# ACT in the order of the program for two of three attention sweeps of a transformer block

## The chip, the cores and the metric

The kernel runs on one core of one Trainium2 chip. The metric is device time in microseconds (us), the median of several executions; the kernel before took 2492.71 us (three runs, 2482.8 to 2496.35). The engines are named as in the profile: PE (TensorE, with PEld for its weight loads), DVE (VectorE), ACT (ScalarE), POOL (GpSimd) and SP (SyncE, which here only issues DMA transfers). Each engine takes its instructions from one queue of its own, in the order in which the built program lists them.

## The reference

All data are float32. The input is x of 2048 rows (tokens) by 1024. With `norm` a layer norm without weights:

```
xn = norm(x)
q, k, v = xn @ wq.T + bq, xn @ wk.T + bk, xn @ wv.T + bv    # each 2048 x 32 heads x 32
scores  = einsum('shd,std->sht', q, k) / sqrt(32)            # 32 x 32 for each token: heads attend to heads
context = einsum('sht,std->shd', softmax(scores), v)
x = x + context
dq = nf4_quant_dequant(w)         # w1, w2: 2752 x 1024, w3: 1024 x 2752
x = x + (silu(norm(x) @ dq1.T) * (norm(x) @ dq2.T)) @ dq3.T
```

`nf4_quant_dequant` works on blocks of 64 weights: it divides by the largest absolute value of the block, replaces each value by the nearest of 16 fixed codes, and multiplies back.

## The kernel before, in words

**The stages.** Three sweeps come first, one for q, one for k and one for v. Each goes over 8 pairs of 128-token tiles, 16 tiles in all. Then a "plain" block of 8 matmul groups (the first weight tile of the feed-forward) is woven with the last context work, and then the feed-forward runs over groups of weight tiles.

**One product.** Every pair of tiles in a sweep is one call of `products` (line 348). It is a Strassen product: seven block products instead of eight. One block product is four matmuls (`mm4`, line 337; the profile shows each fp32 matmul as two records, so eight of them under L339). The sums that Strassen needs are made by letting PE go on accumulating in one PSUM bank `z` and copying it at intermediate points: ACT copies `g0` after the first block product into z, `u2` after the second, `u4` after the third (`copied`, L358); `s7` is a copy of the other bank, `q`. The order on PE is z, q, z, r, z, z (or y), q. PE may not accumulate further into z until the copy of the value before is done. In the first sweep the sixth block product goes to a bank of its own, y, so nothing waits for u4 there; in the other two it goes to z, and ACT copies the end result (`ce`, L383). DVE adds the parts to the two outputs ce and co (L375, L379, L387, L390).

**What else a product carries.** Between block products `fill(n)` puts other work into the program:

- First sweep: PE transposes the normalised x of the next pair (16 transposes `pt`, L471) after the fifth block product, in four groups of four with three PSUM banks. ACT copies each bank twice: to `A` (L474) and, with other strides, to `AV` (L475), which the v sweep will use. DVE forms the Strassen differences of both (L396 to L399), and SP stores them to DRAM (opD, L482; opV, L486). There is one AV buffer: its next copy must wait for the store. DVE also transposes q and adds the bias (L403, L404), and forms Strassen differences of the k and v weights (L516 to L519).
- Second sweep: the scores of the pair before (`sc`, 32 x 32 matmuls in parts of 64, L419), then max, subtraction, exp (ACT, `pr`, L583), sum and scaling.
- Third sweep: the context (`cx`, L433), in parts of 64 matmuls into one PSUM buffer; DVE transposes it back (L652), adds x (L656), SP stores the residual (x1d, L658), and DVE normalises x in the same buffer (L116, L117, L334), which so waits for the store. Two products later PE transposes it (L694), ACT copies that (`xT`, L695), DVE makes differences (`xU`, L710), and SP stores these for the feed-forward.

**The quantiser.** A generator, `background` (line 219), runs through all three stages and the feed-forward. It works on one weight tile of 128 x 1024 after another. A tile has 15 steps. Twelve of them are one ACT activation `sg` (L242) and one DVE operation on `r` (L243); three are DVE alone (L234, L236, L238). There are two sg buffers, so ACT can be at most two steps ahead of DVE. In front of a tile stand an absolute maximum (DVE, L207), a reciprocal (L214, L215) and 16 scalings of 64 columns on ACT (`wn`, L195); at its end 16 more scalings on ACT (`r`, L195). After that the tile is transposed by PE (`ptw`, L161), copied by ACT (`wop`, L162) and stored for the feed-forward (`finish`, line 147). `advance(n)` takes n steps of the generator at that place of the program, `flush` half of a tile's transposes. A product of the first sweep takes 7 steps, one of the third sweep 9. The first feed-forward units need the first tiles; `until` makes sure that they come before.

**What sets the order.** A scheduler orders the instructions of each engine. It takes them from the program, gives each the priority of its place there, and runs a model of the engines: an engine takes whatever instruction is ready, the earliest first. The order that comes out is fixed in the built program. Engines named to `manual_schedule` are excepted: their instructions stay in the order in which the program has them. Before the change that is PE alone, from the beginning to the end. The quantiser's steps depend on little, so where the model sees ACT and DVE idle the scheduler takes them earlier than the program has them.

## Time and profile before

| | us |
|---|---|
| median of three runs | 2492.71 |
| the profiled execution | 2491.25 |
| its span, first to last instruction | 2489.5 |
| PE busy | 2385.8 |
| DVE busy | 1982.1 |
| ACT busy | 1610.2 |
| POOL busy | 279.8 |
| granted clock of PE, mean | 0.987 |

Boundaries in that execution, by PE's first matmul of each stage: first sweep 12.7, second 246.4, third 535.5, plain block 779.5, feed-forward about 832, end 2489.5.

How to read the rows: a timeline row has the start in us from the span's beginning, the duration, the engine, the source line, the operation, the output and input by the program's names (buffer numbers left out), sizes, and how many were merged; in brackets the idle time of the engine before it and what ended it. A row of waits has the engine and what it was to do, whom it waited for, the total in us, how often, and the longest. A waiting engine that isn't PE costs nothing by itself.

### The profile page before, as it was taken

The numbers are of one execution on the slowest core, as the hardware profiler recorded it, in microseconds if no ns is written. First come the engines' busy times: TensorE is split into PE (matmuls) and PEld (weight loads), VectorE is DVE, ScalarE is ACT, GpSimd is POOL, SyncE is SP. The second block draws the span as 40 slices with busy tenths as digits, with TensorE's granted clock in tenths as the row PEclk, the third lists the DMA queues.
The fourth block names the chain that finished last, engine by engine and source line by source line (L and its number), as shares of the span: only waits on it lengthen the run. The fifth ranks groups of instructions, "written<-read, shape, count | busy, mean of one in ns | idle before, by whom it ended". The sixth has DMA issues, their size and how long they took to land.

```text
span 2489.5 us, 36718 instructions
## 1 busy us (share of the span) xinstructions
PE 2385.8 (96%) x14000; PEld 1119.6 (45%) x14000; DVE 1982.1 (80%) x2208; ACT 1610.2 (65%) x3267; POOL 279.8 (11%) x352
## 2 busy tenths in 40 slices
PE   7999999999899999999999999999999999899998
PEld 4444455545455444444444444444444444344433
DVE  7999788878988588989888899898988979871022
ACT  3556544444553378898888988889888888871200
POOL 1010000000000012030120301203012030120300
PEclk8999999999999999999999999999999999999999
DMA  8788643656669587394973939739496394872973
GB/s 309 280 315 327 239 161 116 231 210 218 215 226 324 195 292 166 110 199 148 327 163 119 199 145 323 170 110 207 154 293 174 128 198 157 283 152 72 198 268 138
DMA packets 177297, 513.90 MB, mean 206 GB/s; under 512 B 15904, under 2 KB 70176, under 8 KB 154720
## 3 DMA queue, kind: packets, MB, share of 16 engines
q1 hardware_dynamic: 136224, 438.08, 48.5%
q0 software_dynamic: 40320, 73.42, 18.2%
q8 instruction: 110, 1.80, 0.3%
q14 instruction: 67, 0.55, 0.1%
q10 hardware_dynamic: 576, 0.05, 0.0%
HBM read 283.69 MB, written 227.80 MB: 205 GB/s over the span
## 4 chain that ended last, share of the span: by engine, by line
DVE 18%; issue 17%; ACT 14%; PE 14%; DMA 4%; POOL 1%; DVEq 0%; SPq 0%; POOLq 0%; ACTq 0%
DVE r L243 11%; ACT sg L242 5%; PE z L339 5%; ACT wn L195 4%; PE z L976 4%; DMA x1d<-acc 3%; ACT acc L988 2%; ACT r L195 2%; PE y L976 2%; PE q L339 2%; PE r L976 1%; PE rr L339 1%; POOL x1d L990 1%; DMA out_dram<-acc 1%; ACT wop L162 1%
## 5 line engine op out<-in xcount | busy, mean ns | idle before, releaser
L243 DVE SCALAR_TENSOR_TENSOR r<-sg,r 128x1024 f32<-128x1024 f32 x780 | 945.8, 1214 | 98.1 <-ACT sg L242 66.8
L242 ACT ACTIVATE sg<-wn 128x1024 f32<-128x1024 f32 x780 | 812.4, 1053 | 307.0 <-DVE r L243 286.6
L990 POOL DMA_DIRECT2D x1d<-acc x280 | 244.5, 879 | 1285.7 <-ACT acc L988 1160.8
L339 PE MATMUL z<-xB,w 128*128 128x512 f32 x720 | 324.4, 600 | 5.2 <-ACT u L909 3.7
L339 PE MATMUL z<-xT,w 128*128 128x512 f32 x656 | 296.3, 594 | 5.4 <-ACT u L902 5.4
L339 PE MATMUL q<-xT,w 128*128 128x512 f32 x656 | 291.6, 592 | 0.0
L195 ACT ACTIVATE wn<-wn,rc 128x64 f32<-128x64 f32 x1032 | 267.4, 341 | 22.3 <-DVE rc L215 22.3
L976 PE MATMUL z<-w,h 128*128 128x512 f32 x496 | 236.8, 604 | 2.2 <-DMA w<-wd 1.7
L339 PEld LDWEIGHTS z<-xB,w 128*128 128x128 f32 x720 | 135.4, 192 | 172.4 <-issue 154.7
L339 PEld LDWEIGHTS z<-xT,w 128*128 128x128 f32 x656 | 121.7, 190 | 155.0 <-issue 136.9
L339 PEld LDWEIGHTS q<-xT,w 128*128 128x128 f32 x656 | 123.4, 190 | 149.4 <-issue 146.6
L339 PE MATMUL q<-wT,A 128*128 128x512 f32 x384 | 174.7, 598 | 3.0 <-DVE A L398 3.0
L339 PE MATMUL z<-wT,A 128*128 128x512 f32 x384 | 175.5, 600 | 1.8 <-ACT u L358 1.5
L976 PE MATMUL y<-w,h 128*128 128x512 f32 x320 | 153.9, 599 | 14.7 <-DVE h L963 12.7
L339 PE MATMUL z<-wB,A 128*128 128x512 f32 x320 | 153.0, 623 | 13.4 <-ACT u L358 13.2
L195 ACT ACTIVATE r<-r,am 128x64 f32<-128x64 f32 x608 | 155.1, 341 | 15.6 <-DVE r L243 15.2
L339 PE MATMUL rr<-xB,w 128*128 128x512 f32 x328 | 147.5, 592 | 0.0
L976 PEld LDWEIGHTS z<-w,h 128*128 128x128 f32 x496 | 93.7, 194 | 113.3 <-issue 98.1
L207 DVE TENSOR_REDUCE am<-wn 128x16 f32<-128x1024 f32 (+1 forms) x65 | 78.4, 1206 | 59.0 <-ACT r L195 53.2
L988 ACT COPY acc<-z 128x512 f32<-128x512 f32 x160 | 93.2, 582 | 35.7 <-PE z L976 31.7
L339 PEld LDWEIGHTS q<-wT,A 128*128 128x128 f32 x384 | 72.6, 192 | 91.1 <-issue 84.8
L339 PEld LDWEIGHTS z<-wT,A 128*128 128x128 f32 x384 | 70.4, 190 | 80.7 <-issue 77.1
(132 smaller groups left out, 2591.4 us busy)
## 6 DMA issues: line engine op xcount, KB each, us to landing
x1d<-acc POOLq DMA_DIRECT2D x280, 256.0 KB, 6.1
wd<-wop SPq DMA_DIRECT2D x31, 2048.0 KB, 7.2
w<-wd SPq DMA_DIRECT2D x41, 1280.0 KB, 7.6
wn<-in_w_dram SPq DMA_DIRECT2D x63, 512.0 KB, 4.7
xT<-xdT SPq DMA_DIRECT2D x28, 1024.0 KB, 8.0
xB<-xdB SPq DMA_DIRECT2D x24, 1024.0 KB, 6.1
w<-wd SPq DMA_DIRECT2D x42, 512.0 KB, 5.1
w<-wd SPq DMA_DIRECT2D x10, 1536.0 KB, 7.7
```

What stands on the lines that cost most here:

```text
L162: nc.scalar.copy(o[:q, first + half], pt[:q])
L195: nc.scalar.mul(dst[:, ts(n, BLOCK)], src[:, ts(n, BLOCK)], by[:, n : n + 1])
L207: nc.vector.tensor_reduce(am[:, :nb], v.rearrange("p (b e) -> p b e", e=BLOCK), AX.X, ALU.max, apply_absolute_value=True,)
L242: nc.scalar.activation(t, v, AF.Copy, bias=-edge * by, scale=by)
L243: nc.vector.scalar_tensor_tensor(r, t, code, r, ALU.min, ALU.max)
L339: nc.tensor.matmul(dst, w[:, k, :], xop[:, k, :], start=start and k == 0, stop=stop and k == 3, skip_group_check=True,)
L976: nc.tensor.matmul(dst, side[n][:, ts(q, P)], w3T[g[2 * m]][:, W3[n]], start=start and m == 0, stop=stop and m == 1, skip_group_check=True,)
L988: nc.scalar.copy(t, src)
L990: nc.gpsimd.dma_start(x1d[8 * tbp + 2 * q + j][n], t, accum_op=ALU.add)
```

## The change

A helper `order` is added, which ends the present exception from scheduling and opens a new one for the engines given. It is called four times: PE and ACT before the first sweep, PE alone before the second, PE and ACT before the third, and PE alone before the plain block. So in the first and third sweep ACT executes exactly in the order in which the program is written; in the second sweep, the plain block and the feed-forward the scheduler orders ACT as before. No instruction is added or removed, and no buffer changes. DVE, SP and POOL stay with the scheduler throughout.

```diff
-    ctx.enter_context(tc.manual_schedule(engines={nc.tensor.engine}))
+    by_hand = ExitStack()
+
+    def order(*engines):
+
+        by_hand.close()
+        by_hand.enter_context(tc.manual_schedule(engines={e.engine for e in engines}))
+
+    ctx.callback(by_hand.close)
+    order(nc.tensor, nc.scalar)
...
     sweep.close()
 
 
+    order(nc.tensor)
     sweep, sweep_at = ExitStack(), ExitStack()
...
         A = nextA
 
 
+    order(nc.tensor, nc.scalar)
     def load_x1(i):
...
         advance(2)
         A = nextA
     hook["scale"] = "DVE"
+    order(nc.tensor)
     left.close()
```

## The prediction, made before the changed kernel ran

> **What bounds the kernel now.** The profiled execution took 2491.25 us (span 2489.5); the median of the three runs is 2492.71, and the sum below is added to that median. I read the busy shares first, then the table by stretch (cut where each sweep's first product starts on TensorE), then TensorE's waits, then the order of time around the longest of them.

> ```profile
> PE 2385.8 (96%) x14000; PEld 1119.6 (45%) x14000; DVE 1982.1 (80%) x2208; ACT 1610.2 (65%) x3267; POOL 279.8 (11%) x352
> ```

> ```profile
> 12.70:246.30 233.60, 216.66 (x586) 102.17 (x585) 221.41 (x294) 129.19 (x274) 17.21 (x28) 0.97 0.83 309
> 246.30:535.40 289.10, 281.88 (x4635) 150.04 (x4634) 235.39 (x240) 135.78 (x279) 0.00 (x0) 1.00 0.50 186
> 535.40:746.00 210.60, 195.45 (x3388) 102.23 (x3386) 194.88 (x207) 104.41 (x217) 8.98 (x22) 0.97 0.67 227
> 746.00:832.00 86.00, 78.28 (x1341) 41.72 (x1338) 70.42 (x80) 33.95 (x69) 6.61 (x10) 0.96 0.89 292
> 832.00:2490.00 1658.00, 1606.58 (x4032) 716.77 (x4030) 1255.55 (x1382) 1203.27 (x2427) 244.47 (x280) 0.99 0.67 188
> ```

> Columns are length, then busy PE, PEld, DVE, ACT, POOL, clock, DMA. PE bounds everything, but DVE is nearly as full in the first sweep (221 of 234 us) and the third (195 of 211), and has room in the second (235 of 289). ACT is half idle, so its speed doesn't matter; only what its queue is stopped on does:

> ```profile
> PE z L339 <- ACT u L358: 14.7, 6, 4.3
> ...
> PE pt L471 <- ACT V L475: 12.6, 4, 4.2
> ```

> ```profile
> 615.49 0.57 ACT L358 COPY u<-z 128x512 f32<-128x512 f32 x1
> 622.11 1.06 ACT L242 ACTIVATE sg<-wn 128x1024 f32<-128x1024 f32 x1 [6.05 <-DVE r L243]
> 623.43 1.06 ACT L242 ACTIVATE sg<-wn 128x1024 f32<-128x1024 f32 x1 [0.27 <-DVE r L243]
> 624.76 1.06 ACT L242 ACTIVATE sg<-wn 128x1024 f32<-128x1024 f32 x1 [0.27 <-DVE r L243]
> 625.73 0.57 ACT L358 COPY u<-z 128x512 f32<-128x512 f32 x1
> ```

> ```profile
> 620.95 1.09 PE L694 MATMUL pt<-ident,x 128*128 128x128 f32 x8
> 626.35 5.15 PE L339 MATMUL z<-wB,A 128*128 128x512 f32 x8 [4.30 <-ACT u L358]
> ```

> That is the mechanism. PE accumulates into z and may not go on until ACT has copied it; the copy u stands behind three quantiser steps (sg), and each sg waits for DVE's step two before it. PE loses 4.3 us, and the next four-matmul product takes 4.99 us to its successor instead of the steady 3.43.

> Taking from PE's timeline, start to start, 3.43 us a block product (four matmuls), 2.31 for sixteen transposes, 1.72 and 1.21 for a score or context half, 0.88 for eight later transposes and 0.44 for four weight transposes, PE loses against its own steady pace: first sweep 22.5 us (6.5 of it start-up), second 14.1, third 28.9 up to 779.4, the plain block after it 11.7. Only these 77 us are in play.

> **What the change moves.** PE's and POOL's instruction lists are word for word the same; ACT, DVE and SP hold the same instructions in another order, and from the feed-forward's first unit on (about 832 us) all lists agree again. The last 1658 us cost the same, only shifted. Counting sg instructions on ACT before the first copy (g0) of a product (before to after): 39 to 34 at the first sweep's eighth, 62 to 55 at the second sweep's second, equal from its third to sixth, 97 to 84 at the third sweep's first, 146 to 128 at its eighth, 158 to 158 at the first feed-forward unit. The scheduler runs the quantiser ahead; program order doesn't, and the debt falls due in the second sweep's first two products and the plain block. SP's transfers move with their producers; the ones that anybody waits for are named below (opV and x1d stores), and the weight loads come no later than the steps that read them.

> I followed the new order by hand, with the durations of the rows: sg 1.05, a DVE step 1.21, sixteen scalings 3.93, a PSUM copy 0.58.

> *First sweep, first product.* u2 now stands behind sixteen wn scalings that wait for the reciprocal, which on DVE follows ce. In the trace these run at 34.69 to 38.62; u2 was at 29.84. PE's third z block product (33.07) must wait to about 39.2: +6.1, +2.0 of slow clock. It removes the wait at the transposes (3.96, +1.42), but leaves about 0.5, as the AV copy now waits in line for the opV store (landing 7.8 us). Net +3.2.
> *Second product.* Its wait at the transposes (4.30, +2.45) was sg work ahead of the copies; the eight copies are now contiguous, about 0.5 left. Net -6.3.
> *Third, seventh.* The AV copies wait for the opV store in line: about 2.2 and 2.5 where 0.98 and 2.67 were. Net +1.1.
> *Fourth-sixth.* At the end of the second weight tile sixteen r scalings stand ahead of g0. Their last DVE step follows four 1.22 us query operations: 2.2 (co, late) + 4.7 + 1.2 + 3.9 + 0.6 = 12.6 us after the fifth product's end, where PE needs g0 after 7.3 (two block products and the weight transposes lie between): a wait of 5.3 us, or 3.7 if DVE isn't late. I take 4.3, add 2.0 of slow clock and 0.3 at the next transposes: +6.6, hidden behind nothing. First sweep together: 3.2 - 6.3 + 1.1 + 6.6 = +4.6.

> *Second sweep.* 18 DVE steps, 22 us, instead of 7 fall between two products' ce: in the first u4 is 2.5 late (2.3 before), in the second g0 stands behind an sg whose step is due 3.6 us late, then u2 0.8, +1.4 of clock: +6. DVE's room covers the rest; without it the 11 steps would cost 13. Its end has no sg left, and two waits (1.25 and 2.3) go: -3.5. Together +2.5.

> *Third sweep.* DVE gets 15 steps fewer by the last product's ce (165 for 180). In program order at most three sg stand before u4. In the fourth product the step that the third needs ends at 18.6 us after the product's start and u4 is wanted at 21.2, so the 4 us waits of 620, 660 and 730 don't come. New: at a tile's end the weight transposes wait for the r scalings, 3.3 us (+1.5) once and under 1 twice. The residual's normalisation waits for its x1d store; 4.0 us of other DVE work lie between at the least, near the 3.3 to 4.8 seen, so some tenths each. I take 13 us of loss left of 28.9: -16 (bounds -25, all smooth, and 0, DVE as late as before).

> *Plain block.* 30 sg instead of 12 remain from the eighth g0 on. From the last ce, DVE owes 82.8 us by the rows' means (61.3 before), about 78 as they overlap by some 0.07 us each. The feed-forward's first g0 now stands on ACT behind four scalings that wait for the end of all this: last r product +5.9 +78 +1.7 = 85.6 to 86.2, against 73.8 in the trace (761.3 to 835.1): +12.4, +2 of clock = +14.4. The other bound: DVE was idle for 15.6 of the 86 us in the table, and if the 20 us more were to fill all of that, about +4 would be left. I take the high end, since the order is fixed and the waits for PE's context halves stay in it.

> Sum: 4.6 + 2.5 - 16 + 14.4 = +5.5, so 2492.7 + 5.5 = **2498.2 us**.

> **A rule weighed.** The rows show that waits of PE up to 2.7 us (209.6, 260.1) cost nothing afterwards, and those of 3.2 to 4.5 cost 1.42, 2.45, 1.55, 2.97 and 1.76: 2.0 on average. [...]

> **Rivals.**
> *Slower.* Program order couples ACT to DVE at every copy. If DVE is over 2.6 us late at u4 in the third sweep (18.6 against 21.2), PE waits there too, 4 + 2 us in three products, and the -16 is gone: 2492.7 + 21.5 = 2514. For: DVE is at 93% there now, and my hand count has it 3 to 6 us late by the seventh and eighth products. Against: 15 steps fewer.
> *Faster.* The third sweep runs smooth (-25), and the last burst fits into DVE's 15.6 idle us (+4): 4.6 + 2.5 - 25 + 4 = -14: 2479. For: PE's waits there were all for ACT copies. Against: the ordered chain to the first g0.
> *Nothing moves:* the kernel is on PE for 96% and DVE and ACT have idle time over the whole span, so gains and losses end where they began: 2492.7. It can't be told from mine in a measurement and is counted with it.

> **Chances.** 0.5% is 12.5 us, about what a measurement of this kernel can tell from no change. Mine, with the nothing-rival inside: 0.45, own range 2483 to 2505. Slower: 0.41; each unforeseen wait in one in-order queue adds and none subtracts. Faster: 0.14. The range leaves out a tenth on each side, most of the slower case's width in: **2481 to 2524**.

> **What would show it.** After 832 us the length stays at 1658. A PE wait of about 6 us for u in the first product; one of 4 to 5 for u (or ptw) at the end of the fifth; none of 4 us between 535 and 746; at the plain block's end a PE wait of 5 to 8 us for g, with DVE full to it. Wrong if the 4 us waits reappear in the third sweep, or if the feed-forward's length changes.

## The result, and the profile after

The changed kernel takes 2502.85 us (median of seven runs, 2499.47 to 2506.1), the kernel before beside it 2492.51: a ratio of 1.0045, 95% interval 1.0032 to 1.0058. In a second comparison, made later, it was 2500.25 to 2493.28, ratio 1.0034 (1.0021 to 1.0048). So it is 7 to 10 us slower: less than the 12.5 us (0.5%) that the prediction took for what a measurement can tell, but both intervals lie above 1. Predicted were 2498.2 us and +5.5.

The busy row of the changed kernel, and then its table by stretch with the true starts of its stages: length, busy PE, PEld, DVE, ACT, POOL, clock, DMA share, GB/s.

```profile
PE 2395.9 (96%) x14000; PEld 1122.0 (45%) x14000; DVE 1984.3 (79%) x2208; ACT 1608.6 (64%) x3267; POOL 290.1 (12%) x352
```

```profile
12.80:244.10 231.30, 216.43 (x586) 101.31 (x585) 209.29 (x283) 116.07 (x261) 14.80 (x28) 0.97 0.83 309
244.10:508.80 264.70, 255.49 (x4059) 134.28 (x4057) 213.81 (x216) 115.91 (x221) 0.00 (x0) 0.97 0.49 184
508.80:777.10 268.30, 260.12 (x4554) 136.77 (x4553) 239.22 (x253) 124.83 (x269) 21.31 (x26) 0.99 0.69 236
777.10:835.80 58.70, 47.76 (x747) 25.48 (x746) 57.23 (x63) 37.38 (x67) 7.45 (x6) 0.88 0.78 256
835.80:2498.40 1662.60, 1609.22 (x4033) 717.49 (x4031) 1260.33 (x1389) 1210.87 (x2446) 244.00 (x280) 0.99 0.66 188
```

The same five stretches before were 233.7, 254.1, 279.0, 52.2 and 1657.8 us. The third sweep is 10.7 us shorter, the second 10.6 longer, and the plain block 6.5 longer. In it DVE is now busy for 57.2 of 58.7 us (45.9 of 52.2 before). The last row is 4.8 us longer because the first feed-forward unit still waits for the same steps.

A correction first. The text before the result puts the third sweep's start at 535.5 us. That is the start of this sweep's second product; the sweep begins at 500.5. The table by stretch in the prediction, and its terms for the two sweeps, therefore count one product of the third sweep to the second.

All later readings use one measure: where PE stands at the same place of its list (which is the same in all these kernels), against the kernel before. The four places are the starts of the second sweep, the third sweep and the plain block, and the first unit's third block product (`rr`); before: 246.4, 500.5, 779.5 and 838.5 us, span 2489.5. The differences between neighbouring places give what each stage added (us, one profiled execution each):

| kernel | 1st sweep | 2nd | 3rd | plain, first unit | rest | span | median, ratio (interval) |
|---|---|---|---|---|---|---|---|
| predicted (third sweep from 535.5) | +4.6 | +2.5 | -16 | +14.4 | 0 | +5.5 | |
| changed | -2.3 | +10.6 | -10.7 | +13.3 | -2.0 | +8.9 | 1.0045 (1.0032 to 1.0058) |
| changed, again | -1.8 | +10.9 | -12.0 | +14.2 | +2.0 | +13.3 | 2500.25, 1.0034 (1.0021 to 1.0048) |
| first_only | -3.6 | +11.8 | +0.3 | +1.0 | 0.0 | +9.5 | 2503.32, 1.0039 (1.0024 to 1.0054) |
| third_only | -1.8 | -0.9 | -10.5 | +15.6 | +0.4 | +2.8 | 2491.69, 1.0002 (0.9990 to 1.0014) |
| all_three | -1.4 | +21.1 | -11.8 | +14.3 | -3.0 | +19.2 | 2512.95, 1.0084 (1.0066 to 1.0101) |
| late | -1.9 | +10.4 | -14.6 | +13.6 | -2.6 | +4.9 | 2497.14, 1.0017 (1.0009 to 1.0024) |
| late_store | +5.0 | +8.7 | -14.0 | +14.6 | -4.2 | +10.1 | 2506.54, 1.0060 (1.0047 to 1.0073) |
| plain_too | -0.8 | +11.8 | -13.1 | +13.3 | -0.5 | +10.7 | 2496.55, 1.0021 (1.0012 to 1.0030) |
| third_plain | -0.3 | -0.9 | -12.3 | +13.4 | -3.8 | -3.9 | 2487.03, 0.9983 (0.9973 to 0.9992) |
| third_pass | -1.7 | +2.6 | -15.1 | +3.7 | +14.8 | +4.3 | 2493.04, 1.0002 (0.9993 to 1.0011) |
| third_plain_xu3 | -2.2 | -0.6 | -13.8 | +1.3 | -1.3 | -16.6 | 2476.27, 0.9935 (0.9922 to 0.9949) |
| before_xu3 | +2.1 | -0.2 | +0.8 | -2.1 | -1.1 | -0.5 | 2492.45, 0.9998 (0.9989 to 1.0008) |
| after_xu3 | -2.0 | +10.9 | -13.2 | +8.2 | -0.7 | +3.2 | 2492.42, 0.9999 (0.9989 to 1.0008) |

Five executions whose first sweep has the order of before (third_only, third_plain, third_pass and the two with xu3 that are not of the changed kernel) lie between -2.2 and +2.1 there. A difference of 2 us in one stage is noise.

### The profile page after: what moved, and what is told of

The parts are those of the page before. It is cut to its first block, busy times and chain, and to the rows that moved or that the text cites. A ratio compares the mean times of both kernels' runs of the same rounds, so it can differ in the third digit from the quotient of the medians.

```text
span 2498.4 us, 36700 instructions
## 1 busy us (share of the span) xinstructions
PE 2395.9 (96%) x14000; PEld 1122.0 (45%) x14000; DVE 1984.3 (79%) x2208; ACT 1608.6 (64%) x3267; POOL 290.1 (12%) x352
## 4 chain that ended last, share of the span: by engine, by line
PE 35%; DVE 28%; ACT 15%; issue 14%; DMA 6%; POOL 1%; DVEq 0%; ACTq 0%; SPq 0%; POOLq 0%
DVE r L243 16%; PE z L347 13%; PE q L347 5%; PE z L987 5%; ACT sg L242 5%; ACT wn L195 4%; ACT r L195 3%; PE y L987 2%; DMA x1d<-acc 2%; PE r L347 2%; PE sc L427 2%; ACT acc L999 2%; PE r L987 1%; DMA xdT<-xU 1%; PE rr L347 1%
## 5 line engine op out<-in xcount | busy, mean ns | idle before, releaser
L243 DVE SCALAR_TENSOR_TENSOR r<-sg,r 128x1024 f32<-128x1024 f32 x780 | 945.3, 1213 | 113.0 <-ACT sg L242 80.8
L242 ACT ACTIVATE sg<-wn 128x1024 f32<-128x1024 f32 x780 | 810.5, 1054 | 227.2 <-DVE r L243 205.5
L347 PE MATMUL z<-xT,w 128*128 128x512 f32 x656 | 298.1, 597 | 10.4 <-ACT u L913 5.4
L347 PE MATMUL z<-wT,A 128*128 128x512 f32 x384 | 184.0, 624 | 12.4 <-ACT u L366 5.4
L987 PE MATMUL y<-w,h 128*128 128x512 f32 x320 | 156.7, 608 | 13.1 <-DVE h L974 12.1
```

The source lines that it names most:

```text
L242: nc.scalar.activation(t, v, AF.Copy, bias=-edge * by, scale=by)
L243: nc.vector.scalar_tensor_tensor(r, t, code, r, ALU.min, ALU.max)
L347: nc.tensor.matmul(dst, w[:, k, :], xop[:, k, :], start=start and k == 0, stop=stop and k == 3, skip_group_check=True,)
L987: nc.tensor.matmul(dst, side[n][:, ts(q, P)], w3T[g[2 * m]][:, W3[n]], start=start and m == 0, stop=stop and m == 1, skip_group_check=True,)
```

## The experiments

### The parts alone

first_only leaves out the third call of `order`; ACT is in the scheduler's order from the second sweep on.

```diff
-    order(nc.tensor, nc.scalar)
     def load_x1(i):
```

> ACT in program order in the first sweep alone. My theory: each stage's effect comes from ACT's own order in that stage and the effects add. First sweep -2 as in the changed kernel, the first two products of the second sweep +10 (postponed quantiser steps that the scheduler takes at once), third sweep and plain block as before: +8 us in all, about 2500.5. Rival (coupled): the steps postponed here are missing later too, so the third sweep becomes lighter and the plain block dearer even without the order there: total +2 to +4, with a third sweep that loses 21 instead of 32 us.

third_only begins with PE alone and keeps the third call.

```diff
     ctx.callback(by_hand.close)
-    order(nc.tensor, nc.scalar)
+    order(nc.tensor)
```

> ACT in program order in the third sweep alone. My theory: first sweep as before, no burst at the start of the second (its step counts are those of before), the third sweep -11 (no waits of 4 us for u4), the plain block +13, feed-forward unchanged: +2 us, about 2494.5. Rival (coupled): the third sweep's gain needs the first sweep's postponed steps; then the 4 us waits stay in part and the kernel takes about 2503.

Measured: +11.7 us for first_only and +0.1 for third_only (medians against the kernel before, run beside them). The table shows that the stages add up: first_only has the second sweep's loss (+11.8) and no gain in the third (+0.3); third_only has no loss in the second (-0.9), the third sweep's gain (-10.5) and the plain block's loss (+15.6). The coupled rival is out for both. The changed kernel is slower because of the first sweep's order, whose bill comes in the second sweep; the order in the third sweep gives and takes the same.

### The changed kernel once more

There is no edit.

> The changed kernel once more, beside the kernel before on the same chip, to have both on more runs. My theory: +10.3 as first measured, 1.0045 (between 1.0032 and 1.0058). Rival: the first comparison, from 7 runs each, was high, and the true figure is that of the variants that share its third sweep and plain block (1.0017 to 1.0021): +4 to +6.

Measured 1.0034, within the first interval. PE's timeline agrees with the first execution within 1.5 us a stage up to the feed-forward.

### The second sweep in program order

all_three leaves out the second call, so that ACT is in program order in all three sweeps.

```diff
     sweep.close()
-    order(nc.tensor)
     sweep, sweep_at = ExitStack(), ExitStack()
```

> The changed kernel with ACT in program order in the second sweep too (all three sweeps). My theory: the +10 at the second sweep's start is the burst of 15 steps before its second product's g0; in program order there are 5, so the loss goes: -10 against the changed kernel, with the plain block's burst unchanged, about 2493. Rival: the loss there comes from what the first sweep leaves behind (stores and weight loads that come late), so it stays, and program order brings waits of its own in the softmax chain: 2503 or more.

It takes 2512.95 us. The theory was right on the burst: against PE's steady pace, the second sweep's first two products lose 0.9 and 4.9 us instead of 4.4 and 8.7. It was wrong on the rest, where the rival's waits in the softmax chain cost more. PE's waits in this sweep, all_three:

```profile
PE ptw L161 <- ACT r L195: 7.6, 2, 6.5
PE z L347 <- ACT g L366: 7.5, 2, 4.1
```

The order of time on ACT around the 6.5 us wait (PE wants `ptw` from 377.0):

```profile
381.96 1.06 ACT L591 ACTIVATE pr<-pr 128x1024 f32<-128x1024 f32 x1 [8.45 <-DVE pr L585]
382.92 3.91 ACT L195 ACTIVATE r<-r,am 128x64 f32<-128x64 f32 x16
```

The exponential stands 8.45 us at the head of ACT's queue for DVE's subtraction, and the scalings that PE waits for stand behind it. Behind the first sweep in program order, the scheduler's order is the better one in the second sweep.

### The first product

late takes the generator's first step of the first product behind u2.

```diff
-            advance(0 if n == 5 else 1)
+            advance(0 if n == 5 or p == 0 and n == 7 else 2 if p == 0 and n == 6 else 1)
```

> The changed kernel with the first product's first generator step (absolute maximum, reciprocal, 16 scalings wn) one place later in the program, behind u2 instead of ahead of it; nothing else of ACT's order changes. My theory (u2 behind the scalings is what PE's third z product waits for): the 5.6 us wait and its 1.6 us of slow clock go, nothing of them comes back, 7 us less than the changed kernel, about 2496, and later stages keep their offsets. Rival: the scalings then stand ahead of u4 and the transposed x, and PE loses the same at the 16 transposes: 2502.

late_store adds to it that the first product's AV differences and their store stand ahead of that product.

```diff
+        if p == 0:
+            now.finished_v()
         cs = products(now.A, fill, (lambda name: None) if more else next_W("k"), ps_t)
...
-        now.finished_v()
+        if p > 0:
+            now.finished_v()
```

> The kernel of late, with the first product's differences of AV and their store (opV) put ahead of that product in the program, so that the store starts some 6 us sooner. My theory: in the first product three waits stand behind one another and only the last one counts; with the scalings gone it is the AV copy's wait for the store (6.4 us and 1.7 of slow clock at the 16 transposes). It goes, and the second product's start comes 7 to 8 us earlier than in late (about 46 instead of 53.8 us), the total 2490. Rival: ACT is still held at the scalings or the store is no sooner, since DVE and the DMA queues are full there: less than 3 us, 2495 or more.

ACT in late, from u2 to the first AV copy:

```profile
29.86 0.59 ACT L366 COPY u<-z 128x512 f32<-128x512 f32 x1 [6.78 <-PE z L347]
34.25 3.93 ACT L195 ACTIVATE wn<-wn,rc 128x64 f32<-128x64 f32 x16 [3.80 <-DMA xt<-in_x_dram]
...
43.68 0.59 ACT L483 COPY AV<-pt 128x512 f32<-128x512 f32 x1 [3.44 <-DVE st L116]
```

u2 is free (29.86), as the theory said, and PE doesn't wait for it. But the AV copy then waits until 43.68 (the operation named as its releaser, a statistic on x, has nothing to do with AV; the opV store, issued at 37.75 us, lands about then, by the 5.8 us that such a store took in late_store), and PE loses 6.4 us at the transposes and 1.7 of slow clock: the rival. The second product starts at 53.8 us, in the changed kernel at 53.3. In late_store the store starts at 34.3 and is no longer what holds the copy; but DVE's reciprocal comes 3.1 us later behind the AV differences, and the copies of the transposed x (from 42.8 us) now stand behind the scalings:

```profile
37.39 3.93 ACT L195 ACTIVATE wn<-wn,rc 128x64 f32<-128x64 f32 x16 [6.90 <-DVE rc L215]
```

The second product starts at 53.6, and it then loses another 7.2 us, its AV copy waiting 4.20 us for the next store. The changed kernel and two remedies have three different waits there and one end. The theory of late_store fell, to the first half of its rival. Open: late loses 6.1 us against the kernel before beside it, the changed kernel 7.0 and 10.3, although late's first product is no shorter; the one trace has the difference in the third sweep and later, the intervals overlap in part, and nothing here explains it.

### The plain block

plain_too keeps program order through the plain block and the first unit's first block product.

```diff
     hook["scale"] = "DVE"
-    order(nc.tensor)
     left.close()
...
     now = Unit(*units.pop(0))
     now.first()
+    order(nc.tensor)
```

> The changed kernel with ACT kept in program order through the plain block and the first feed-forward unit's first block product. 17 quantiser steps instead of 30 then stand before that unit's g0. My theory: the loss of 13 at the plain block was these 13 steps, taken by the scheduler earlier than anybody needs them; the next units have room for them (9 and 10 steps where 0 and 6 were, 12 are usual), so -12 against the changed kernel, about 2491. Rival: the debt is real and only put off: the same 12 us are lost in the first three units instead, 2502, with waits for u or g between 840 and 915 us.

third_plain is the same with third_only's first line, that is without the first sweep's order.

> ACT in program order in the third sweep, the plain block and the first feed-forward unit's first block product; the first and second sweep as before. In the built order 8 sg and 10 scalings r still stand ahead of the first g0, since instructions of the units behind it are filled in. My theory, mended: what counts is not how many steps are done in all but what stands directly ahead of g0. Third sweep -11 to -16; at the plain block a wait for g0 of 5 us or more stays: total 2486 to 2491, no better than 3 to 5 us below third_only. Rival (count alone: 145 steps instead of 158 are enough): no wait at g0, 2478.

plain_too measured 2496.55, between the theory and its rival; its profiled execution (2501.97 us) is a long one. Fewer steps were not enough. ACT around the first g0 in plain_too (g, L905):

```profile
840.07 2.49 ACT L195 ACTIVATE r<-r,am 128x64 f32<-128x64 f32 x10 [0.68 <-DVE r L243]
842.47 0.56 ACT L905 COPY g<-z 128x512 f32<-128x512 f32 x1
```

PE had finished with z at 833.8 and wanted the copy by 837.1. ACT had stood idle for 14.5 us up to 819.6, but the scheduler, which may put later instructions between those of a fixed order, put eight sg and then these ten scalings between the last copy of the transposed x (828.4) and g0. The theory that fewer steps ahead of g0 are enough fell, and third_plain's mended one held: 2487.03, no better than 4.7 us below third_only, with PE waiting 6.01 us for g0.

third_pass keeps program order to the end of the feed-forward's first pass (edit against third_plain).

```diff
     now = Unit(*units.pop(0))
     now.first()
-    order(nc.tensor)
...
         hs = {}
+        if n == 0:
+            order(nc.tensor)
```

> As third_plain, but ACT stays in program order to the end of the feed-forward's first pass (its first four weight tiles). 138 sg instead of 158 stand before the first g0, with a single one directly ahead of it. My theory (the loss at the plain block is the quantiser steps that the scheduler pulls ahead of the first g0): neither the wait for the normalised x nor that for g0 comes, plain block and first unit lose 12 like before instead of 28, and the third sweep's gain is kept: -14 against third_only, about 2478, 0.5% under the kernel before. Rival: program order makes waits of its own in the first pass, first at u2 of the first unit, where 16 scalings and 4 steps stand ahead: 5 to 8 us there, about 2485 or more.

With one sg ahead of g0, the wait for g0 is gone, and plain block and first unit cost +3.7 instead of +15.6. But 2493.04 us is the rival's side: the pass itself loses 14.8. PE's longest waits there in total, third_pass:

```profile
PE z L347 <- ACT u L912: 3.8, 2, 1.9
```

The row is u2 behind scalings and steps, as in the first sweep; behind it come 3.6 us for `h`, 3.0 for another copy u and 2.1 for weight transposes. And the wait for the normalised x (3.3 us) is still there, with no quantiser step on DVE ahead of it. So it had another cause. DVE in third_plain ahead of that wait:

```profile
807.65 0.69 DVE L720 TENSOR_TENSOR xU<-xT,xU 128x512 f32<-128x512 f32 x1 [4.33 <-DMA xdT<-xU]
808.26 1.95 DVE L662 STREAM_TRANSPOSE cx<-cx 128x1024 f32<-128x1024 f32 x1
```

xU has two buffers, and DVE stands still for their stores (2.78 us at the one before, 4.33 here) with the last context's transposition behind it. third_plain_xu3 is third_plain with a third buffer for xU, and one for mx instead of two, for room.

```diff
-            u[n + 1] = work.tile([P, 4, P], FP, tag="xU", name="xU", bufs=2)
+            u[n + 1] = work.tile([P, 4, P], FP, tag="xU", name="xU", bufs=3)
...
-        mx = small.tile([P, 4, 8], FP, tag="mx", name="mx")
+        mx = small.tile([P, 4, 8], FP, tag="mx", name="mx", bufs=1)
```

> third_plain with three buffers for xU instead of two (and one for mx instead of two, to make room, which is used in the second sweep only). Six sg steps and no scalings r now stand directly ahead of the first g0 (8 and 10 before). My theory: in the plain block DVE stood still 2.8 and 4.3 us for stores of xU, with the last context's transposition behind it; that was the wait for the normalised x (3.9 us, and about 2.7 of slow clock); it goes for the most part, and the wait for g0 falls by 3: 8 us less than third_plain, about 2479. Rival: the stores themselves are late because the DMA engines are 80% busy there, so the wait for x stays and only the 3 us at g0 go: 2484.

Measured 2476.27 us, 0.9935 (0.9922 to 0.9949): faster than both kernels. DVE and PE in third_plain_xu3:

```profile
798.31 0.69 DVE L720 TENSOR_TENSOR xU<-xT,xU 128x512 f32<-128x512 f32 x1 [2.85 <-DMA xdT<-xU]
800.67 1.98 DVE L662 STREAM_TRANSPOSE cx<-cx 128x1024 f32<-128x1024 f32 x1 [1.67 <-PE cx L441]
```

```profile
808.40 1.04 PE L704 MATMUL pt<-ident,x 128*128 128x128 f32 x8
809.28 3.60 PE L347 MATMUL z<-xB,w 128*128 128x512 f32 x8
...
819.71 3.70 PE L347 MATMUL z<-xT,w 128*128 128x512 f32 x8 [3.40 <-ACT g L905]
```

The transposition now waits for PE alone, the transposes of x follow without a gap, and only 3.4 us at g0 are left. The order ahead of g0 moved too: six sg stand there, not eight and ten scalings, so the smaller wait at g0 isn't the buffer's doing alone. The third sweep's gain is kept for once: plain block and first unit cost +1.3. The third buffer without the order past the plain block (on third_only) was not run.

The same buffer in the kernel before and in the changed one (same edit):

> The kernel before with three buffers for xU and one for mx, and its order left to the scheduler. My theory: the third buffer helps only where ACT's order leaves DVE free of quantiser steps in the plain block; in the kernel before, x waits 0.6 us there, so 0 to -3 us against before, 2490 to 2493. Rival: the buffer makes the gain of third_plain_xu3 by itself (third product's residual, stores): -8 us or more, 2485 or less.

> The changed kernel with three buffers for xU and one for mx. Three sg then stand directly ahead of the first g0 behind 16 scalings, 155 instead of 158 in all, so the plain block is still filled with quantiser steps. My theory: in the changed kernel it is these steps on DVE that hold x and g0 up, not the stores of xU, so most of the loss of 13 in the plain block and first unit stays: 0 to -5 against the changed kernel, 2496 to 2501. Rival: the stores of xU hold them up here as well: -8 or more, 2492 or less.

before_xu3 is 0.9998: the buffer by itself gives nothing, as the theory said. after_xu3 is 0.9999, 8 to 10 us below the changed kernel in the medians, where at most 5 were expected: the rival's size, but not its reason. The trace shows half of each: the wait for x stayed, that for g0 did not. PE in after_xu3:

```profile
828.23 1.94 PE L704 MATMUL pt<-ident,x 128*128 128x128 f32 x8 [4.33 <-DVE x L342]
...
838.94 3.70 PE L347 MATMUL z<-xT,w 128*128 128x512 f32 x8 [1.43 <-ACT g L906]
```

The scheduler's order changed with the buffer: three sg stand directly ahead of g0, with all sixteen scalings ahead of these (831.16 us), and no longer four scalings that start at 842.74. How many of the 8 to 10 us this explains stays open; the profiled execution has 5 to 6 of them in this stage.

## Why the prediction was right or wrong

The sign of the total was right, and its size within a factor of two (+5.5 foreseen, +10.3 and +7.0 measured). But by the prediction's own boundaries three of its five terms were off, by -6.9, +9.2 and +4.2 us, and the first of these errors hid half of the other two. That the total came so near is in part luck. Both intervals lie above no change, so the rival in which nothing moves is out as well.

**First sweep, +4.6: measured about -2.** The first product is right: u2 stands behind the scalings, the wait is 5.44 us where 6.1 was predicted. ACT (u2 follows at 38.49) and then PE, changed kernel:

```profile
34.66 3.93 ACT L195 ACTIVATE wn<-wn,rc 128x64 f32<-128x64 f32 x16 [11.17 <-DVE rc L215]
```

```profile
39.11 3.44 PE L347 MATMUL z<-wT,A 128*128 128x512 f32 x4 [5.44 <-ACT u L366]
```

The net was +2.2 at the second product's start (+3.2 predicted), and the second product lost 6.8 us less (6.3 predicted; beside the steps that the prediction named, sixteen scalings had stood ahead of its copies). The sixth lost 6.0 (6.6 predicted), by the same mechanism, ACT (g0 follows at 170.53) and PE:

```profile
166.70 3.93 ACT L195 ACTIVATE r<-r,am 128x64 f32<-128x64 f32 x16 [6.94 <-DVE r L243]
```

```profile
171.15 5.40 PE L347 MATMUL z<-wT,A 128*128 128x512 f32 x8 [2.05 <-ACT g L366]
```

The weight transposes ahead of this block product wait for the same scalings, so it comes 4.2 us late in all (4.3 predicted), and 1.8 of slow clock follow.

The step that failed is "third, seventh: +1.1". It took the losses there (1.0 and 2.9 us) for waits of the AV copies for the opV store, and added to them. But ACT doesn't stand still at these copies in the kernel before; what delays PE is how many entries of ACT's queue stand ahead of the copy that it wants. ACT and PE in the third product, before:

```profile
102.00 1.57 ACT L474 COPY A<-pt 128x512 f32<-128x512 f32 x3
103.43 0.63 ACT L475 COPY V<-pt 128x512 f32<-128x512 f32 x1
```

```profile
104.12 0.66 PE L471 MATMUL pt<-ident,xn 128*128 128x128 f32 x4 [1.32 <-ACT V L475]
```

and in the changed kernel:

```profile
97.47 0.59 ACT L482 COPY A<-pt 128x512 f32<-128x512 f32 x1
98.08 0.58 ACT L483 COPY AV<-pt 128x512 f32<-128x512 f32 x1
```

```profile
98.72 0.66 PE L479 MATMUL pt<-ident,xn 128*128 128x128 f32 x4 [0.45 <-ACT AV L483]
```

The scheduler had put three A copies and V first, and PE went on behind V; in program order A and AV alternate, and PE goes on behind the second copy. In the seventh product seven scalings (1.78 us) stood ahead of the copies as well. Both losses went: -3.9 where +1.1 was predicted. The store is waited for in neither product of the changed kernel: in the third it was issued at 91.3 us instead of 95.8 and landed at 98.0, in the seventh at 203.8 instead of 202.9.

**Second sweep, +2.5: measured +11.7 and +11.8 in the window meant (246 to 535 before).** The place was right: the first two products, u4 and then g0 and u2 late. That the first sweep's order is the cause, first_only shows. The size was wrong. The waits that reach PE in the changed kernel:

```profile
263.95 5.38 PE L347 MATMUL z<-wB,A 128*128 128x512 f32 x8 [2.50 <-ACT u L366]
...
284.20 5.40 PE L347 MATMUL z<-wT,A 128*128 128x512 f32 x8 [2.88 <-ACT g L366]
```

Waits of 2.5 (2.5 predicted) and 2.9 us (3.6 predicted), each with a slow block product behind it (5.4 us where 3.6 is the row's usual), and a third at 302 us. The term that was mis-sized first is the slow clock: I had charged 1.4 us for all this, since waits up to 2.7 us had cost nothing before; 5.1 us came (1.8, 1.8 and 1.5). The start of the sweep cost 9.9, not 6. And of the 3.5 us to be gained at the sweep's end, one came: the wait of 2.3 us at the third sweep's first product became one of 1.8 with 1.7 us of slow clock.

**Third sweep, -16: measured -11.8 and -12.8 in the window meant (535 to 779 before).** PE's waits in the sweep held 12.6 us for u before:

```profile
PE z L339 <- ACT u L358: 12.6, 5, 4.3
```

In the changed kernel there is no such row, and the largest is:

```profile
PE sc L427 <- issue: 1.6, 1, 1.6
```

The slow rival needed DVE 2.6 us late at u4. It wasn't: ACT was 0.76 us ahead of PE at the fourth product's u4 (second row), though DVE's step had kept it 3.97.

```profile
625.60 1.06 ACT L242 ACTIVATE sg<-wn 128x1024 f32<-128x1024 f32 x1 [3.97 <-DVE r L243]
627.41 0.58 ACT L366 COPY u<-z 128x512 f32<-128x512 f32 x1 [0.76 <-PE z L347]
```

So the margin was a third of the hand count's. The wait at a tile's end came as predicted (3.4 us and 1.7 of slow clock, predicted 3.3 and 1.5). Not foreseen were the eighth product's small losses, 4.9 us where 1.9 were. The term was mis-sized by 4 us: of 13 us of loss predicted, 17 were left.

**Plain block, +14.4: measured +13.3 and +14.2.** PE at its end, before:

```profile
827.33 1.06 PE L694 MATMUL pt<-ident,x 128*128 128x128 f32 x8 [0.40 <-DVE x L334]
...
835.10 3.60 PE L339 MATMUL z<-xT,w 128*128 128x512 f32 x8
```

and in the changed kernel:

```profile
829.03 1.94 PE L704 MATMUL pt<-ident,x 128*128 128x128 f32 x8 [5.25 <-DVE x L342]
...
844.33 5.32 PE L347 MATMUL z<-xT,w 128*128 128x512 f32 x8 [4.93 <-ACT g L906]
```

The chain to g0 on ACT there:

```profile
842.74 1.06 ACT L195 ACTIVATE wn<-wn,rc 128x64 f32<-128x64 f32 x4 [2.43 <-DVE rc L215]
```

The end of the chain is where it was put: four scalings behind the reciprocal, DVE full to it (2.43 us of ACT's wait end with it), and g0 at 843.7. It is the time of g0 that the sum gave, and that was right; that PE would spend it in two waits, for x and for g0, the prediction did not say. What the experiments add: the number of postponed steps doesn't set this bill. The changed kernel has 158 sg ahead of g0; third_plain with 145 still pays +13.4, third_plain_xu3 with 143 pays +1.3 and nothing behind it. third_pass, with 138, pays +3.7 here, but 14.8 later, in waits of its own.

**Feed-forward, 0: measured -2.0 and +2.0.** Right.

**The slow clock.** The prediction took its own rows (nothing after waits up to 2.7 us, 2.0 us on average after those of 3.2 to 4.5) for a limit on the length of one wait. No run shows such a limit, and the rows above contradict it: the block product took 5.40 us after a wait of 2.05, which that limit has free, and 3.70 after one of 3.40 in third_plain_xu3, which it charges with 2.0. What the traces show in its place is in the last section.

## What to carry to other kernels

Where engines feed one another through in-order queues, as here, fixing one engine's order moved work rather than removing it (-10.7 us in the third sweep, +13.3 behind it): follow the displaced steps to the place where the next scheduled region takes them up, and look at what stands directly ahead of the first copy that the matrix engine waits for there, not at how many steps are done in all. The gain of one stage was kept here when the next hand-over was mended too (the order kept past the hand-over and one more buffer: 0.9935, where the order alone gave 0.9983 and the buffer alone nothing). Before a loss is called a wait for a transfer, look whether the engine named stands still there: at the third and seventh products it was busy with other entries of its queue. And before a wait is taken away, name the one right behind it: at the first product the changed kernel and two remedies ended within 0.5 us of one another.

## What the runs showed of the hardware

A wait's length alone didn't say here whether PE was slow after it. The same wait of 2.50 us, at the same place of the program, was followed by a block product of 5.38 us in the changed kernel (263.95, above) and by one of 3.70 in late_store:

```profile
271.21 3.70 PE L347 MATMUL z<-wB,A 128*128 128x512 f32 x8 [2.50 <-ACT u L366]
```

```profile
260.53:263.94 3.41, 0.93 (x3) 0.10 (x1) 3.10 (x4) 2.63 (x4) 0.00 (x0) 1.00 1.13 435
263.95:267.36 3.41, 3.41 (x4) 1.51 (x5) 2.78 (x3) 3.24 (x11) 0.00 (x0) 0.50 0.88 362
```

```profile
267.11:270.52 3.41, 1.60 (x4) 0.38 (x2) 3.20 (x4) 2.46 (x3) 0.00 (x0) 1.00 1.09 453
270.53:273.94 3.41, 2.73 (x7) 1.29 (x8) 3.31 (x4) 3.24 (x10) 0.00 (x0) 1.00 0.95 390
```

In the changed kernel nearly the whole wait lies in one window, PE is busy for 0.93 of its 3.41 us, and the next window has a clock of 0.50. In late_store the wait is cut in two, PE is busy for 1.60 and 2.73 us, and the clock stays at 1.00.

A count over the traces of the kernel before and the changed kernel, with PE's idle time as the profile gives it, agrees. Before, PE was idle for 0.57 to 1.00 of the window in the 15 windows at full clock whose next one was slow, and for 0.52 or less in the other 694. In the changed kernel 15 windows at full clock were idle for 0.61 or more, and the next was slow after each; of the four between 0.55 and 0.59, after two; of the 688 with 0.47 or less, after four, which were idle for 0.31 to 0.46 and all hold weight transposes or the 32 x 32 matmuls of the scores; why those differ wasn't found. An estimate from these figures, for windows that hold block products of this kernel alone: a wait of less than 1.9 us (0.57 of 3.41) brings no slow clock, a wait of more than 4.2 (twice 0.61 of 3.41) brings some, and between them it depends on where the wait lies against these windows. In the changed kernel's sweeps the slow clock after the waits told above cost 1.5 to 1.8 us each; half of a window of 3.41 us is 1.7.
